# Two fused convolution layers on one core: x1's and x3's stores while layer 0 runs alone, and an image's first value rows

## The chip, the cores and the metric

The kernel runs on one core of a Trainium2 chip. The metric is the device time of one execution in microseconds (us). A profiled execution of the kernel gives the trace that the views below are read from. The engines are named PE (TensorE, matmuls; PEld its weight loads), DVE (VectorE), ACT (ScalarE), POOL (GpSimd) and SP (SyncE, which here only issues DMAs). SPq and ACTq in a view are the queues of instructions of these engines.

## The reference, cut to what matters

Layer 0 normalises each image by groups, makes three 1x1 convolutions of it, computes nine weights per position from two of them, and sums nine shifted copies of the third (x3) with these weights. Layer 1 is local attention over 7x7 windows of keys and values with reflected borders, beside a dynamic 3x3 convolution. Both are added to their input.

```python
# layer 0: x is (8, 256, 64, 64)
x1 = _conv1x1(x, w1, b1); x2 = _conv1x1(x, w2, b2); x3 = _conv1x1(x, w3, b3)
...
w = _conv1x1(h, cw2, cb2).reshape(B, G, K * K, H, W)
x3p = jnp.pad(x3, ((0, 0), (0, 0), (1, 1), (1, 1)))
x3u = _unfold3(x3p).reshape(B, G, SHARE, K * K, H, W)
out = jnp.einsum('bgskhw,bgkhw->bgshw', x3u, w).reshape(B, OUT, H, W)
...
# layer 1, attention part
v = _c1x1(x, Wv, bv).reshape(b * HEAD, HD, h, w)
uv = _unfold(jnp.pad(v, rpad, mode='reflect'), KA).reshape(b * HEAD, HD, kk, n)
...
out_att = jnp.einsum('bnk,bdkn->bdn', att, uv).reshape(b, c, h, w)
...
x = x + _L0_conv_ref(_gn(x), ...)
x = x + _L1_conv_ref(_gn(x), ...)
```

The result of layer 0 with its residual, before layer 1, is called x1 in the kernel (another x1 than in the reference).

## The kernel before, in words

An image has 8 bands of 8 rows; 8 images make 64 bands. The main loop runs over `g` from -12 to 63 and in each over eight steps `s`. In stage `g`, layer 1 works on band `g`, and layer 0 on bands ahead: its 1x1 convolutions on band `g + 12`, its hidden maps on `g + 11`, its products on `g + 10`. For `g < 0` there is no layer 1 work, and layer 0 runs alone: twelve such stages come first (products are in their alone form up to `g = -2`). Image `b + 1` follows image `b` without a break: its first value rows are made in the last stage (`i == NB - 1`) of image `b`, or in stage -1 for the first image.

The order of the instructions is written out by hand. `beside` (L914) puts functions on two lists of a step, `mid` and `end`, which the loop calls at the middle and at the end of it. `steer` (L984) issues most loads at the step's start. `after(n, f)` calls `f` when `n` places have passed; a step has six places. Each engine takes its instructions in the order in which they were written, and an instruction that waits holds all that stand behind it on its engine. SP issues all DMAs of the main loop.

The layer 0 part of a stage, by names and lines:

- `value_maps` (L362) makes x3: PE's matmuls into `p3`, ACT's copy with bias into `x3n` (one buffer for each half of the channels), and a store to DRAM (L375). While alone it is called at s = 2 and s = 3.
- `values_by_group` (L381) loads x3 back by groups into `x3q` (two buffers), five or six DMAs at s = 5, one of which (L397) needs the next band's x3. `x_by_group` (L399) loads the band's x into `xg` by four DMAs at s = 4. `load_x` (L99) fetches x for the convolutions (`xc`, s = 0) and for the statistics of a later image (`xs`, s = 3).
- `tap_weights` (L459) makes the nine products on DVE (L479, tile `prod`, two buffers). While alone, six of them are added into `xg` by POOL (L487) and three are summed by PE (`gather`, L500), and `combine` (L507) on DVE adds PE's sum. `take` (L509) then takes the statistics of the result and stores x1 to DRAM by four DMAs (L519). In the order of the program, `combine` of a band stands on DVE directly behind the first product of the next band, and `take` runs about s = 2 of the next stage.

The layer 1 part that is touched: `load_rows` (L547) loads a band's rows of x1 with three rows above and below, `yp`, and `normalise` scales them on ACT. `values` (L575) makes a tile row of values on PE from them, in two halves, copied by ACT into `vc` (one buffer, L600). `store_values` (L607) stores it to the DRAM tile `vd` (lines L616 to L625), 14 DMAs for the first tile row of an image and 8 for most others. `value_tile` (L627) loads one of four column tiles `vt` (11 buffers) of a tile row from there (L642). For tile rows 0 and 8 the reflected rows have no row of their own in `vd`: each is loaded from the row that it mirrors, so a tile takes 4 x 2 DMAs where others take 2. `weighted_values` (L786) multiplies probabilities by the value tiles on PE, one to two steps after the scores; band `i` needs tile rows `i` and `i + 1`. At an image's boundary, tile row 0 is made at s = 4 and 5 of the last stage and loaded at the end of s = 7; tile row 1 is made at s = 6 and 7 and loaded at the ends of s = 0, 1 and 2 of the next.

Of the kernel before, what the change touches and what calls it, by code (L numbers as in the profile page):

```python
# [18 lines left out]
P = 128  # L19
# [4 lines left out]
R = 8  # L24
BAND = R * W
NB = H // R
# [21 lines left out]
PAD = KA // 2  # L48
WP = W + 2 * PAD
TQ = 8  # L50
# [3 lines left out]
KW = TQ + 2 * PAD  # L54
# [32 lines left out]
def conv_layers_kernel(ctx: ExitStack, tc: tile.TileContext, ins: dict, out: bass.AP):  # L87
    nc = tc.nc
# [48 lines left out]
    x3n = [const.tile([P, R, HP], F32, name=f"x3n_{ct}") for ct in range(NCT)]  # L137
# [72 lines left out]
    images = [Image() for b in range(B)]  # L210
# [148 lines left out]
        if i == NB - 1:  # L359
            nc.gpsimd.tensor_copy(t[0:96, R + 1, :], t[0:96, R - 1, :])  # L360

    def value_maps(b, i, mt):  # L362

        im = images[b]
        if mt == 0:
            im.x3[i] = dram.tile([C, R, HP], F32, tag="x3", name=f"x3_{b}_{i}")
        p3 = ps.tile([P, BAND], F32, tag="gen", name=f"p3_{b}_{i}_{mt}", bufs=4)
        for kt in range(NCT):
            nc.tensor.matmul(  # L369
                p3, im.w3s[:, kt, mt * P : (mt + 1) * P], im.xc[i][:, kt, :],  # L370
                start=(kt == 0), stop=(kt == NCT - 1),
            )
        p3 = p3.rearrange("p (r c) -> p r c", r=R)
        nc.scalar.activation(x3n[mt][:, :, 1 : 1 + W], p3, AF.Identity, bias=im.bias[:, 1 + mt : 2 + mt])
        nc.sync.dma_start(out=im.x3[i][mt * P : (mt + 1) * P], in_=x3n[mt])  # L375

    def pieces(v, q):

# [80 lines left out]
    def tap_weights(b, i, u, alone, at):  # L459


        im = images[b]
        first, n = TG[alone] * u, min(TG[alone], KK - TG[alone] * u)
        pw = ps.tile([P, n, SR * HP], F32, tag="gen", name=f"pw_{b}_{i}_{u}", bufs=4)
        for j in range(n):
            nc.tensor.matmul(  # L466
                pw[:, j], c2[:, first + j], h2n[i % 2].rearrange("p r c -> p (r c)"), start=True, stop=True
            )

        def product(j):  # L470
            k = first + j
            if alone and j == n - 1:
                prod = w1.tile([P, NCT, RP, W], F32, tag="yp", name=f"prod_{b}_{i}_{k}", bufs=3)
                prod = prod.rearrange("p t r c -> p (t r c)")[:, : SHARE * SR * HP]
                prod = prod.rearrange("p (s n) -> p s n", s=SHARE)
            else:
                prod = w0.tile([P, SHARE, SR * HP], F32, tag="prod", name=f"prod_{b}_{i}_{k}", bufs=2)
            at = k // 3 * HP + k % 3
            nc.vector.scalar_tensor_tensor(  # L479
                prod[:, :, :RUN], pw[:, j, :RUN].unsqueeze(1).to_broadcast([P, SHARE, RUN]),  # L480
                par[:, PCB2 + k : PCB2 + k + 1],
                im.x3q[i].rearrange("p s r c -> p s (r c)")[:, :, at : at + RUN], ALU.add, ALU.mult,
            )
            if alone and j == n - 1:
                after(9, lambda: gather(prod))
            else:
                nc.gpsimd.tensor_add(im.xg[i], im.xg[i], rows(prod))  # L487
            if k == KK - 2 + (not alone):
                if alone:
                    after(13, combine)  # L490
                after(14 if alone else 7, take)

        def rows(v):
            return v.rearrange("p s (r c) -> p s r c", c=HP)[..., :W]

        def gather(prod):
            if u == 0:
                im.part = score_tile(f"sum_{b}_{i}").rearrange("p t (s r c) -> p t s r c", r=SR, c=W)
            for t in range(2):
                nc.tensor.matmul(  # L500
                    im.part[:, t], ident, rows(prod)[:, t * SHARE // 2 : (t + 1) * SHARE // 2],
                    start=(u == 0), stop=(u == KK // n - 1),
                )

        def combine():
            x = im.xg[i].rearrange("p s r c -> p (s r c)")
            nc.vector.tensor_add(x, im.part.rearrange("p t s r c -> p (t s r c)"), x)  # L507

        def take():  # L509
            x = im.xg[i]  # L510
            if i == 0:
                im.st1 = stat.tile([P, 2 * NB, 6], F32, tag="st1", name=f"st1_{b}")
            for t in range(2):
                v = x[:, t * SHARE // 2 : (t + 1) * SHARE // 2].rearrange("p s r c -> p (s r c)")
                nc.vector.bn_stats(im.st1[:, 2 * i + t, :], v)
            t = im.x1[i] = dram.tile([C, BAND], F32, tag="x1", name=f"x1_{b}_{i}")
            for q in range(NQR):
                v = x[q * REL : (q + 1) * REL].rearrange("p s r c -> p s (r c)")
                nc.sync.dma_start(out=pieces(t, q), in_=v)  # L519

        for j in range(n):
            after(at[j], lambda j=j: product(j))


    def norm_rows(b):
        im = images[b]
# [80 lines left out]
    def store_values(b, j):  # L607
# [9 lines left out]
        for d in range(1, PAD + 1):  # L617
            for to, c in ((PAD - d, d), (PAD + W - 1 + d, W - 1 - d)):
# [3 lines left out]
                else:  # L622
                    for p in range(2):
                        o = vd[at + p : at + p + 2 * count[p] - 1 : 2, to : to + 1].rearrange("u c n -> c u n")
                        nc.sync.dma_start(out=o, in_=vc[p * W + c : p * W + c + 1, : count[p]])  # L625

    def value_tile(b, j, u):  # L627


        im = images[b]  # L630
        vd = im.vd[j]
        vt = im.vt[j, u] = w1.tile([CHUNK, 2, C], F32, tag="vt", name=f"vt_{b}_{j}_{u}", bufs=11)
        if j == 0:
            runs = [(PAD, PAD, R - PAD)] + [(PAD - d, PAD + d, 1) for d in range(1, PAD + 1)]
        elif j < NB:
            runs = [(0, 0, R)]
        else:
            runs = [(0, 1, PAD)] + [(PAD - 1 + d, PAD - d, 1) for d in range(1, PAD + 1)]
        for to, at, n in runs:
            for g in range(2):  # L640
                c0 = (2 * u + g) * TQ
                nc.sync.dma_start(  # L642
                    out=vt[to * KW : (to + n) * KW, g], in_=vd[at : at + n, c0 : c0 + KW]
                )

    def new_keys(i):

# [266 lines left out]
    def beside(g, s):  # L914

        b, i = divmod(g, NB)
        bn, inx = divmod(g + 1, NB)
        mid, end = [], []
# [15 lines left out]

        made = [(b, i + 2, 4)] if g >= 0 and i < NB - 1 else []
        if i == NB - 1 and 0 <= b + 1 < B:
            made = [(b + 1, 0, 4), (b + 1, 1, 6)]
        for bb, j, d in made:
            if s in (d, d + 1) and (j < NB or s == d):
                mid.append(lambda bb=bb, j=j, d=d: values(bb, j, s - d))  # L940
            if s == d + 1:
                end.append(lambda bb=bb, j=j: store_values(bb, j))
            if s == 7 and d == 4:
                for u in range(NT // 2):
                    end.append(lambda bb=bb, j=j, u=u: value_tile(bb, j, u))
        if g >= 0 and i == 0 and s in (0, 1, 2):
            for u in {0: (0,), 1: (1,), 2: (2, 3)}[s]:
                end.append(lambda u=u: value_tile(b, 1, u))

        nxt = [(b, i + 2, 0)] if g >= 0 and i + 2 < NB else []  # L950
        if i == NB - 1 and 0 <= b + 1 < B:
# [7 lines left out]
        alone = g < 0  # L959
        if 0 <= g + AHEAD < B * NB:  # L960
            bq_, iq = divmod(g + AHEAD, NB)
            if alone and s == 0:
                mid.append(lambda: small_maps(bq_, iq, small_tile(f"{bq_}_{iq}"))())
            if s == (2 if alone else 0):
                (mid if alone else end).append(lambda: value_maps(bq_, iq, 0))
            if s == (3 if alone else 1):
                mid.append(lambda: value_maps(bq_, iq, 1))
        if 0 <= g + AHEAD - 1 < B * NB and s == (2 if alone else 1):
            bh, ih = divmod(g + AHEAD - 1, NB)

# [6 lines left out]
        if 0 <= g + AHEAD - 2 < B * NB and s in TAPS_AT[g < -1]:  # L977
            u = TAPS_AT[g < -1].index(s)
# [5 lines left out]
    def steer(g, s):  # L984

        b, i = divmod(g, NB)
        if s == (2 if g >= 0 else 3) and i == NB - 2 and 0 <= b + 1 < B:
            norm_rows(b + 1)
        n = g + AHEAD + 1
        if s == 2 and n % NB == 0 and 0 < n < B * NB:  # L990
            scaled_weights(n // NB)
        if s == (3 if g < -1 else 7) and g + AHEAD0 < B * NB:
            first_stats(*divmod(g + AHEAD0, NB), n=40 if g < -1 else 9)
        if s == 5 and 0 <= g + 1 < B * NB:
            bn, inx = divmod(g + 1, NB)
            xr = images[bn].xr[inx] = x_tile("xr", bn, inx)
            nc.sync.dma_start(out=xr, in_=images[bn].x1[inx].rearrange("(t p) n -> p t n", p=P))
        if s == (0 if g < 0 else 4) and 0 <= g + 1 + AHEAD < B * NB:
            bn, inx = divmod(g + 1 + AHEAD, NB)
            if inx not in images[bn].xc:  # L1000
                images[bn].xc[inx] = load_x(bn, inx, "xc")
        if s == 5 and 0 <= g - 1 + AHEAD < B * NB:
            values_by_group(*divmod(g - 1 + AHEAD, NB))
        if s == 4 and 0 <= g - 1 + AHEAD < B * NB:
            x_by_group(*divmod(g - 1 + AHEAD, NB), g < -2)

    with tc.manual_schedule():

        for i, use in enumerate(("xc", "xc", "xr", "xr", "xs", None, None, None)):
# [4 lines left out]
            x = first_stats(0, i, use, t)  # L1014
# [167 lines left out]
```

## Time and profile before

| | |
|---|---|
| median of 3 runs | 4012.74 us (4012.72 to 4017.47) |
| the profiled execution | 4010.67 us |
| its span, first to last instruction | 4008.9 us |
| busy: PE, DVE, POOL, ACT | 95%, 85%, 79%, 71% of the span |
| first scores of layer 1 (PE, L737) | at 246.34 us |
| layer 0 alone, 27.0 to 247.7 us: PE, DVE, POOL, ACT busy | 172.4, 158.9, 150.7, 98.4 of 220.7 us |
| layer 0 alone: mean DMA share, traffic | 0.85, 213 GB/s |
| 300 to 700 us: PE busy, DMA share | 391.1 of 400 us, 0.44 |

How to read it: a view gives an instruction by its line in the kernel, engine, operation and tiles, with numbers left out of the tiles' names, so that `x3` and `x1` in DRAM both appear as `x`, and `p3` as `p`; the line tells them apart. In a timeline a row has start, duration, engine, line, operation, `out<-in`, and how many of them were merged (`x4`); square brackets hold the engine's idle time before it and what ended that. In the page's groups the number ahead of the last bar is the busy time, and behind it stands the idle time of the engine before these instructions with its main cause. A DMA row on SPq is the issue; the data land later.

### The profile page before, as it was taken

Reading aid. Unit: us, or ns where it says so; the run is one execution under the profiler, and the core shown is the slowest. Engines: PE = TensorE matmul, PEld = TensorE weight load, DVE = VectorE, ACT = ScalarE, POOL = GpSimd, SP = SyncE. Lnnn points to the kernel's source line nnn. Section 1 sums busy time; section 2 is a strip of 40 time slices with the busy share of each in tenths; the row PEclk is TensorE's granted clock in tenths of the full one; section 3 lists DMA queues with packets and bytes.
Section 4 is the critical chain, followed back from the end, with each engine's and each line's share of the span. In section 5 each row is a group of like instructions: output and inputs, shape, how many; then the busy total and the mean of one; then the engine's idle time right before and its main releaser. Section 6 shows DMA issues by size and latency. Waiting matters only on the chain.

```text
span 4008.9 us, 72420 instructions
## 1 busy us (share of the span) xinstructions
PE 3807.0 (95%) x24620; PEld 2116.9 (53%) x24620; DVE 3419.8 (85%) x7143; ACT 2839.5 (71%) x6779; POOL 3174.8 (79%) x2156
## 2 busy tenths in 40 slices
PE   6879999999999999999999999999999999999998
PEld 3445555555555555555555555555555555555554
DVE  5868988888888988888988888978988889977888
ACT  3457777677676777777777677777777677676776
POOL 4758988788987988878887888978888888965665
PEclk9989999999999999999999999999999999999999
DMA  8864543544444443444443544444443544322220
GB/s 230 201 165 113 134 114 104 136 125 113 127 115 122 124 124 101 125 132 120 124 115 104 138 125 118 110 130 124 118 115 90 129 116 104 85 61 88 71 65 32
DMA packets 493171, 469.42 MB, mean 117 GB/s; under 512 B 68432, under 2 KB 394624, under 8 KB 492544
## 3 DMA queue, kind: packets, MB, share of 16 engines
q1 hardware_dynamic: 489472, 460.23, 43.4%
q10 hardware_dynamic: 3328, 4.55, 0.3%
q8 instruction: 195, 3.19, 0.3%
q14 instruction: 176, 1.44, 0.1%
HBM read 325.64 MB, written 138.99 MB: 116 GB/s over the span
## 4 chain that ended last, share of the span: by engine, by line
PE 27%; POOL 26%; DVE 22%; ACT 10%; issue 7%; DMA 5%; SPq 3%; POOLq 0%; DVEq 0%; ACTq 0%
PE pf L873 13%; POOL xg L487 13%; POOL ex L1080 6%; DVE prod L479 5%; DVE acc L856 5%; DVE rec L894 4%; PE small L786 3%; ACT x L343 3%; PE sco L737 2%; PE ptp L774 2%; ACT ex L878 2%; DVE prob L751 2%; DMA x3q<-x 2%; PE pq L672 2%; DVE acc L830 2%
## 5 line engine op out<-in xcount | busy, mean ns | idle before, releaser
L873 PE MATMUL pf<-yp,c_wfc 128*128 128x512 f32 x4096 | 1917.1, 597 | 6.2 <-ACT ex L878 5.1
L487 POOL TENSOR_TENSOR xg<-xg,prod 128x1024 f32<-128x1024 f32 x549 | 1200.7, 2187 | 177.2 <-DVE prod L479 148.3
L873 PEld LDWEIGHTS pf<-yp,c_wfc 128*128 128x128 f32 x4096 | 744.0, 191 | 730.3 <-issue 647.1
L1080 POOL TENSOR_TENSOR ex<-ex,ex 128x1024 f32<-128x1024 f32 x384 | 907.9, 2364 | 55.9 <-ACT ex L878 51.8
L479 DVE SCALAR_TENSOR_TENSOR prod<-pw,c_par,x3q 128x1040 f32<-128x1040 f32 x576 | 737.9, 1288 | 124.8 <-PE pw L466 56.1
L830 DVE SCALAR_TENSOR_TENSOR acc<-yp,c_chan,acc 128x504 f32<-128x504 f32 (+3 forms) x1104 | 775.0, 702 | 50.7 <-ACT acc L821 30.3
L856 DVE SCALAR_TENSOR_TENSOR acc<-hid,c_chan,acc 128x504 f32<-128x504 f32 (+3 forms) x1024 | 749.8, 732 | 18.1
L878 ACT ACTIVATE ex<-pf 128x512 f32<-128x512 f32 x1024 | 602.1, 588 | 204.2 <-PE pf L873 184.3
L759 ACT ACTIVATE prob<-prob,nmax 128x196 f32<-128x196 f32 x1024 | 459.2, 451 | 217.1 <-DVE nmax L751 216.9
L768 ACT ACTIVATE prob<-prob,tot 128x196 f32<-128x196 f32 x1024 | 413.0, 452 | 235.3 <-DVE tot L766 235.1
L895 POOL TENSOR_TENSOR tot<-tot,rec 128x256 f32<-128x256 f32 x254 | 185.4, 730 | 412.9 <-DVE rec L894 387.9
L894 DVE RECIPROCAL rec<-tot 128x256 f32<-128x256 f32 x256 | 445.9, 1742 | 17.2 <-POOL tot L889 12.3
L776 ACT COPY pt<-ptp 112x512 f32<-112x512 f32 x511 | 294.8, 577 | 123.4 <-PE ptp L774 122.3
L751 DVE CUSTOM_DVE_ANT_0 prob<-sco,c_mask 128x196 f32<-128x196 f32 x1024 | 324.5, 354 | 20.4 <-PE sco L737 20.2
L786 PE MATMUL small<-pt,vt 112*64 112x64 f32 x8144 | 300.3, 226 | 37.5 <-DMA vt<-vd 37.1
L774 PEld LDWEIGHTS ptp<-ident,prob 128*112 128x112 f32 x2044 | 228.1, 134 | 188.9 <-issue 135.2
L774 PE MATMUL ptp<-ident,prob 128*112 128x128 f32 x2044 | 322.9, 281 | 1.3 <-ACT vc L600 1.3
L786 PEld LDWEIGHTS small<-pt,vt 112*64 112x64 f32 x8144 | 261.5, 138 | 116.7 <-issue 75.4
L737 PE MATMUL sco<-kb,qb 64*64 64x196 f32 x4096 | 236.1, 343 | 39.6 <-DVE kb L708 32.9
L592 PE MATMUL pv<-c_wv,yp 128*128 128x256 f32 (+1 forms) x1056 | 252.8, 382 | 2.6 <-ACT ex L878 2.1
L369 PE MATMUL p<-xc,w3s 128*128 128x512 f32 x512 | 248.4, 609 | 7.0 <-ACT ex L878 7.0
L466 PEld LDWEIGHTS pw<-h2n,c_c 128*128 128x128 f32 x1152 | 173.3, 191 | 153.5 <-issue 113.1
(139 smaller groups left out, 4756.9 us busy)
## 6 DMA issues: line engine op xcount, KB each, us to landing
vt<-vd SPq DMA_DIRECT2D x448, 112.0 KB
x<-x3n SPq DMA_DIRECT2D x128, 264.0 KB
x3q<-x SPq DMA_DIRECT2D x128, 264.0 KB
xc<-in_x SPq DMA_DIRECT2D x64, 512.0 KB
xg<-in_x SPq DMA_DIRECT2D x256, 128.0 KB
x<-xg SPq DMA_DIRECT2D x256, 128.0 KB
yp<-x SPq DMA_DIRECT2D x128, 256.0 KB
xr<-x SPq DMA_DIRECT2D x64, 512.0 KB
```

Source lines behind the costliest of these rows:

```text
L479: nc.vector.scalar_tensor_tensor(prod[:, :, :RUN], pw[:, j, :RUN].unsqueeze(1).to_broadcast([P, SHARE, RUN]), par[:, PCB2 + k : PCB2 + k + 1],
L487: nc.gpsimd.tensor_add(im.xg[i], im.xg[i], rows(prod))
L759: nc.scalar.activation(prob[:, h, :NKEY], prob[:, h, :NKEY], AF.Exp, bias=nmax[:, h : h + 1], scale=-1.0, accum_out=tot[:, h : h + 1],)
L768: nc.scalar.activation(prob[:, h, :NKEY], prob[:, h, :NKEY], AF.Copy, scale=tot[:, h : h + 1])
L774: nc.tensor.transpose(ptp[:, h, ch], prob[:, h, ch * CHUNK : (ch + 1) * CHUNK], ident)
L786: nc.tensor.matmul(po[half[h], :, t * TQ : (t + 1) * TQ], im.vt[i + ch, m][:n, t, (2 * ct + h) * HD : (2 * ct + h + 1) * HD], pt[:n, h, ch ...
L830: nc.vector.scalar_tensor_tensor(o, yp[:, ct, ra + dr : rb + dr, ca + dc : cb + dc], chan[:, ct, CW1 + k : CW1 + k + 1], o, ALU.mult, ALU.add,
L856: nc.vector.scalar_tensor_tensor(o, hid[:, ra + dr : rb + dr, ca + dc : cb + dc], chan[:, ct, CW2 + k : CW2 + k + 1], o, ALU.mult, ALU.add,)
L873: nc.tensor.matmul(pf, wfc[:, kt, 2 * m + j, ct * P : (ct + 1) * P], images[b].yp[i][:, kt, PAD : PAD + R], start=(kt == 0), stop=(kt == N ...
L878: nc.scalar.activation(ex[:, j].rearrange("p (r c) -> p r c", r=R), pf, AF.Exp)
L894: nc.vector.reciprocal(rec, v)
L1080: after(4, lambda ex=ex, exb=exb: nc.gpsimd.tensor_add(ex, ex, exb))
```

## The change

- `take` no longer stores x1 itself. The new function `keep` does; while alone it is put on a list `held`, which `steer` empties at s = 6, behind the loads of s = 3, 4 and 5. Otherwise it is called at once, as before.
- For `g < 0`, x3's stores are issued by ACT instead of SP.
- An image's tile rows 0 and 1 of values are made one step sooner (s = 3 and 4, 5 and 6).
- The new function `mirror_rows` copies three rows within the DRAM tile `vd` for tile rows 0 and 8, one step after `store_values`; `value_tile` then loads every tile by two DMAs.
- The tiles of tile row 1 are loaded in the middle of s = 0 and of s = 2, two at a time.

```diff
-    def value_maps(b, i, mt):
+    def value_maps(b, i, mt, alone):
...
-        nc.sync.dma_start(out=im.x3[i][mt * P : (mt + 1) * P], in_=x3n[mt])
+        queue = nc.scalar if alone else nc.sync
+        queue.dma_start(out=im.x3[i][mt * P : (mt + 1) * P], in_=x3n[mt])
...
                 nc.vector.bn_stats(im.st1[:, 2 * i + t, :], v)
+            if alone:
+                held.append(keep)
+            else:
+                keep()
+
+        def keep():
+            x = im.xg[i]
             t = im.x1[i] = dram.tile([C, BAND], F32, tag="x1", name=f"x1_{b}_{i}")
...
+    def mirror_rows(b, j):
+
+        vd = images[b].vd[j]
+        for d in range(1, PAD + 1):
+            to, at = (PAD - d, PAD + d) if j == 0 else (PAD + d, PAD - d)
+            nc.sync.dma_start(out=vd[to], in_=vd[at])
+
     def value_tile(b, j, u):
...
-        if j == 0:
-            runs = [(PAD, PAD, R - PAD)] + [(PAD - d, PAD + d, 1) for d in range(1, PAD + 1)]
-        elif j < NB:
-            runs = [(0, 0, R)]
-        else:
-            runs = [(0, 1, PAD)] + [(PAD - 1 + d, PAD - d, 1) for d in range(1, PAD + 1)]
-        for to, at, n in runs:
-            for g in range(2):
-                c0 = (2 * u + g) * TQ
-                nc.sync.dma_start(
-                    out=vt[to * KW : (to + n) * KW, g], in_=vd[at : at + n, c0 : c0 + KW]
-                )
+        at, n = (0, R) if j < NB else (1, 2 * PAD)
+        for g in range(2):
+            c0 = (2 * u + g) * TQ
+            nc.sync.dma_start(out=vt[: n * KW, g], in_=vd[at : at + n, c0 : c0 + KW])
...
-            made = [(b + 1, 0, 4), (b + 1, 1, 6)]
+            made = [(b + 1, 0, 3), (b + 1, 1, 5)]
...
-            if s == 7 and d == 4:
+            if s == d + 2 and j in (0, NB):
+                end.append(lambda bb=bb, j=j: mirror_rows(bb, j))
+            if s == 7 and j != 1:
...
-        if g >= 0 and i == 0 and s in (0, 1, 2):
-            for u in {0: (0,), 1: (1,), 2: (2, 3)}[s]:
-                end.append(lambda u=u: value_tile(b, 1, u))
+        if g >= 0 and i == 0 and s in (0, 2):
+            for u in (s, s + 1):
+                mid.append(lambda u=u: value_tile(b, 1, u))
...
+        if s == 6:
+            while held:
+                held.pop(0)()
```

## The prediction

> **What bounds the kernel now.** I read the page first, for where TensorE (PE) is not full.
>
> ```profile
> span 4008.9 us, 72420 instructions
> ...
> PE   6879999999999999999999999999999999999998
> ...
> L786 PE MATMUL small<-pt,vt 112*64 112x64 f32 x8144 | 300.3, 226 | 37.5 <-DMA vt<-vd 37.1
> ```
>
> A slice is 100 us. PE is full from the fourth on, so there only PE's idle time can be won; the largest wait is for value tiles, 37.1 us. The first two and a half slices, layer 0 alone, are not full. Next the windows view, cut at the starts of the DVE `combine` (L507), one per alone stage (columns: stretch, length, busy us and instructions of PE, PEld, DVE, ACT, POOL, clock, DMA share, GB/s):
>
> ```profile
> 71.33:90.24 18.91, 14.99 (x71) 6.91 (x70) 16.91 (x15) 7.57 (x15) 14.03 (x12) 0.91 0.87 198
> ...
> 108.81:126.95 18.14, 13.46 (x68) 6.88 (x69) 14.70 (x16) 6.44 (x13) 13.78 (x10) 0.91 0.86 191
> ...
> 182.23:199.93 17.70, 13.23 (x63) 6.36 (x64) 14.69 (x15) 5.21 (x12) 14.23 (x11) 0.81 0.84 192
> 199.93:220.22 20.29, 17.24 (x83) 8.82 (x82) 17.54 (x27) 7.82 (x16) 14.86 (x11) 0.92 0.96 239
> ```
>
> Six stages from 90.24 to 199.93 take 109.69 us, 18.28 each, and no engine is busy over about 15. The timelines of SP's queue and of DVE in one of them say why:
>
> ```profile
> 110.05 2.56 SPq L519 DMA_DIRECT2D x<-xg  x4
> 112.65 0.61 SPq L99 DMA_DIRECT2D xs<-in_x  x1
> 113.36 0.43 SPq L375 DMA_DIRECT2D x<-x3n  x1
> 113.83 2.69 SPq L405 DMA_DIRECT2D xg<-in_x  x4
> ...
> 120.46 0.61 SPq L397 DMA_DIRECT2D x3q<-x  x1
> ...
> 125.73 1.30 DVE L479 SCALAR_TENSOR_TENSOR prod<-pw,c_par,x3q 128x1040 f32<-128x1040 f32 x1 [1.93 <-DMA x3q<-x]
> 126.95 1.21 DVE L507 TENSOR_TENSOR xg<-sco_sum,xg 128x1024 f32<-128x1024 f32 x1
> ```
>
> It is a ring: x1's stores wait for the combine (ended 110.03); xs, x3's store, xg and x3q queue behind them on SP; the first product waits for x3q; the next combine stands behind that product on DVE. Last, the image boundary, SP's timeline and PE's:
>
> ```profile
> 729.30 17.12 SPq L642 DMA_DIRECT2D vt<-vd  x32
> 746.53 1.33 SPq L616 DMA_DIRECT2D vd<-vc  x2
> 747.90 3.83 SPq L621 DMA_DIRECT2D vd<-vc  x6
> 752.41 1.44 SPq L642 DMA_DIRECT2D vt<-vd  x2
> ```
> ```profile
> 755.32 0.55 PE L786 MATMUL small<-pt,vt 112*64 112x64 f32 x8 [2.61 <-DMA vt<-vd]
> ```
>
> The 32 small loads of tile row 0 hold SP for 17 us, so row 1's tiles come too late. The PE waits view, image by image, gives 8.9 us in the first image and 2.9, 4.1, 4.1, 5.1, 3.5, 2.6, 5.8 in the other seven, 28.1 together.
>
> [...] an x3 store costs SP 0.34 us, and the DMA row is full for about 15 of these 18 us. [...] So each row copy holds SP until its source row has landed; before shows the like once, ScalarE's copy waiting 11.87 us for `vd<-vc` at 245.25. [...] No copy within DRAM is in this trace.
>
> **Part 1, x1's stores and x3's stores while layer 0 is alone.** SP's order per stage becomes xc, xs, xg x4, x3q, then x1 x4; ScalarE issues x3's. Removed ahead of x3q: 2.56 + 0.43 us of issue and, more, the wait for the combine. xs then waits only for its statistics (DVE at 122.52), three places before the combine. What is late next? Three candidates.
> - POOL with DVE. From a combine's start: combine, two statistics, two products, then POOL's five adds; at 108.81 the adds began 5.09 us later and took 11.19, so 16.3 and a handover. The stage at 71.33 checks it: 18.91, with one 2.28 us DVE preparation of `c_wfc` in this chain, gives 16.63. I take 16.6.
> - DMA. In the half-microsecond DMA row of 108 to 128 the engines stand at 8 to 9 tenths from about 111.2 to 126: 14.8 us of work per stage. A floor just below, so x3q lands with little to spare: xs, xg, x3q and x3's stores are some 2.4 MB, 10 us at 240 GB/s, with 13 between the statistics and the product after next.
> - PE, 14.4 us dense from its gather at 94.13 to 108.5.
>
> ScalarE gains two issues of 0.34 us and the wait for the end of its own 0.69 us activation: some 2 us on 6 to 10 of 18; the hidden maps queued behind it reach PE's convolution 8 us before PE takes them (108.2 against 116.05). Free.
> Sum: six stages at 16.6, plus 1.5 us for the statistics of the next image inside the one at 145.30 (DVE 16.24 against 14.7), 101.1: **8.6 us off**. Bounds: 0 if DMA, fuller, is late all the same; 14 if POOL's gap closes too. The stage at 199.93 follows the normalisation chain, and stages before 71 wait for weights and the first x3q: nothing.
>
> **Part 2, values one step sooner, first image.** Today the 14 stores of tile row 0 are issued from 233.41 to 244.03, behind x3q; ScalarE's next values copy waits 11.87 us for them, the reflected keys stand behind it, and PE idles 6.45 us at 246.3. A step sooner, the first values matmul waits for the normalised rows (ScalarE, 222.8); the second half follows near 228, the stores run 230 to 240, landing 1.6 (the measured `vd<-vc`), scores at 242.7: **3.6 off** (0 to 6). x3q, now behind the stores, is needed only inside the next stage.
>
> **Part 3, whole-tile loads and copies of reflected rows.** Per image two tile rows go from 32 loads to 8: SP sheds 2 x 24 x 0.54 = 26 us, and gets 2 x 3 copies of 72 KB. A copy's cost has no row: below, 1.6 us to landing; above, on one engine (240/16 = 15 GB/s) 4.9 us each and in series with landings about 23 us for three. [...]
> SP from the end of step 4 at the boundary (708.5 in the trace above: a step before 716.57): stores 9.2, xr and x3q 4.5, copies 5, second stores 5.2, xs and x1 3.3, eight tile loads 5.2, the first four of row 1 2.6, landing 2: all in by about 37 us, near 745. PE wants them at 751.9. The wait goes, with 6 us to spare. What is late next: the values matmul, a step sooner, meets the normalised rows with 1.8 us of slack (ScalarE done at 697.97, PE there at about 699.8), 0 in the last image; I allow 0.5 us per boundary. PE holds the same work otherwise, so idle removed is time removed: 28.1 - 3.5 = **24.6 off**. In the first image the row-1 tiles come some 20.6 us after the first scores against 19.3 wanted: **7.6** of 8.9 off. Bounds for this part: 15 to 37. The earlier place for row 1's loads costs SP at most a wait for the weighing before it, under 1 us in the waits view.
>
> **Sum.** 8.6 + 3.6 + 7.6 + 24.6 = 44.4. Profiled execution: 4010.67 us (span 4008.9 and 1.8 around it), so 3966.3. The median is 2.1 above that execution, so 3968 for a median; I say 3967.
>
> **Rivals.**
> - A, as above: 3967, own range 3952 to 3982. Chance 0.50.
> - B, alone stages unmoved: DMA is the bound (share 0.86), x3q only trades queueing behind x1 for queueing in the DMA engines. For it, the DMA row; against, 2 us of idle rings each stage and 16.6 measured. Only 32 us go: 3980. Chance 0.22.
> - C, more than that: earlier tiles and rows also let ScalarE off its waits for `yp` (63.7 us in all, up to 10.5, behind the same SP bursts), and the alone stages run at 15.5. Another 8 + 10: 3949. Against it, PE shows no wait of that kind. Chance 0.15.
> - D, slower: the row copies hold SP. Three in series on one engine are 23 us, 18 over what I took and 12 beyond the 6 to spare: PE waits 12 us at eight boundaries, 96, against 49 that were to go or came from elsewhere (37.1 + 3.6 + 8.6): +47, 4059. It turns slower when SP is held about 17 us in all (8 x 6.2 against 49). [...] Chance 0.06.
> - E, no change: the boundary wait goes over to another engine and the stages stay: about 4010. Chance 0.07. That the change does not do what it says I see nowhere: the stores are moved only for stages below zero, but tiles and copies work in every image.
>
> A measurement of this kernel tells about 0.2% (8 us) from no change. Faster: A, B, C, 0.87. Same 0.06, slower 0.07. Range 3940 to 3994: A, B, C and what lies between; D and E are left out.
>
> **What would show it.** Right: combines 16.3 to 17 us apart; x1 x4 after x3q on SP; no row L786 waiting for `vt<-vd` over 2 us in all but the first image; vt bursts of 8 in some 5 us; scores of the first band about 12 us sooner. Wrong: products still waiting for x3q (B); a copy taking over 5 us, SP standing before tile loads (D); PE waiting at `pv` for `yp`.

## The result, and the profile after

The changed kernel takes 3972.22 us (median of 4 runs, 3969.72 to 3973.63) against 4012.73 (4 runs of the kernel before beside it, 4010.49 to 4017.47): a ratio of 0.9896, with a 95% interval of 0.988 to 0.9911. The prediction said 3967 with a range of 3940 to 3994. The time came out as predicted; its parts did not. They missed in opposite directions, so that the agreement of the sum is luck. That is what the experiments are about.

The profiled execution took 3969.72 us. The page, in the parts shown of before:

```profile
span 3967.9 us, 71908 instructions
...
PE   5879999999999999999999999999999999999998
...
L795 PE MATMUL small<-pt,vt 112*64 112x64 f32 x8144 | 294.9, 225 | 1.3 <-DMA vt<-vd 0.9
```

The wait for value tiles is gone (37.1 us before, 0.9 now), and the span is 41 us shorter. But in the first of the forty slices PE has fallen from 6 tenths to 5: layer 0's alone part has become slower. To split the two I use PE's first scores of layer 1 (`sco<-kb,qb`), which begin at 246.34 us before and at 254.20 after. Up to there the changed kernel **loses 7.9 us** (predicted: 12.2 won, parts 1 and 2 together). From there to the end of the span it takes 3713.7 us against 3762.6: it **wins 48.9** (predicted: 32.2, part 3). The sum, 41.0, is close to the 44.4 predicted because the two misses, 20.1 and 16.7, nearly cancel.

The stages of the alone part, in the windows view cut at the starts of the DVE `combine` (L508 now; columns as in the prediction):

```profile
93.93:113.24 19.31, 16.50 (x76) 7.52 (x74) 14.71 (x14) 8.96 (x17) 14.47 (x14) 0.91 0.70 190
...
132.57:150.68 18.11, 13.67 (x58) 6.76 (x59) 15.10 (x17) 4.02 (x8) 13.23 (x7) 0.72 0.86 198
150.68:171.57 20.89, 19.07 (x104) 10.14 (x102) 16.23 (x27) 12.37 (x26) 14.37 (x13) 1.00 0.72 186
```

The six stages that took 109.69 us take 115.43, from 93.93 to 209.36. DVE and POOL are busy for the same 13 to 16 us in each, and the DMA share (the last but one column) is lower than before, 0.70 to 0.86 where it was 0.76 to 0.91. So rival B, to which the DMA engines were the bound, does not explain it: something is waiting to issue. The timeline of SP's queue shows where:

```profile
108.23 6.90 SPq L527 DMA_DIRECT2D x<-xg  x4
117.49 0.37 SPq L99 DMA_DIRECT2D xc<-in_x  x1
117.96 0.41 SPq L99 DMA_DIRECT2D xs<-in_x  x1
118.56 2.56 SPq L406 DMA_DIRECT2D xg<-in_x  x4
...
124.43 2.40 SPq L390 DMA_DIRECT2D x3q<-x  x3
```

x1's four stores do stand behind the loads, as intended. But they take 6.90 us where four issues had taken 2.56, and then xc waits until 117.49. What SP waits for is in the waits view of its queue, from 60 to 225 us (columns: us in all, times, longest):

```profile
SPq L527 <- DMA x<-x3n: 30.8, 6, 9.4
SPq L406 <- DMA x<-x3n: 16.4, 4, 5.5
SPq L99 <- DMA x<-x3n: 12.8, 5, 5.0
```

Together 60.0 us, and none of it in the same view of the kernel before. `x<-x3n` is x3's store, which ScalarE now issues. Yet x1's store (L527) reads only xg, and the xg and xs loads (L406, L99) only the input: they have no data in common with x3. In that stage ScalarE's own timeline has:

```profile
111.87 0.33 ACTq L376 DMA_DIRECT2D x<-x3n  x1
...
114.37 0.33 ACTq L376 DMA_DIRECT2D x<-x3n  x1
```

SP goes on two to three microseconds after each of them, at 113.93 and 117.49. The trace shows what joins them: it has the semaphores that are waited for ahead of each DMA, and the one to which the DMA reports its landing. The 2878 DMAs of the changed kernel report to eight semaphores, 100 to 107, and both SP's and ScalarE's are found on all eight. In all 2870 cases in which an earlier DMA had the same semaphore, it had landed before the next was issued. SP takes the eight in turn: 2808 of 2837 steps from one of its DMAs to its next go to the next number. From 60 to 225 us 16 steps leave one out, and these are the 16 numbers that ScalarE's stores of x3 from 77.02 to 208.65 have. An excerpt for the stage above, ScalarE's queue first, then SP's, with the time of issue:

```
L376 x3's store, first half    waits 103, 109 (ScalarE)   reports to 103   111.87
L376 x3's store, second half   waits 105, 109 (ScalarE)   reports to 105   114.37

L527 x1's store, third         waits 103                  reports to 103   113.93
L99  xc                        waits 105, 110 (PE)        reports to 105   117.49
```

In all 15 of the waits summed above, the DMA before which SP stands reports to a semaphore that one of ScalarE's stores of x3 took last, and SP goes on 0.01 to 0.15 us after that store has landed.

My reading: when all of these were on SP, the DMA that had the semaphore last had always been issued, and in most cases had landed: before, 153 of SP's 159 DMAs from 60 to 225 us found it landed, and the other six stood 0.87 us at most for it. Now it may be one that ScalarE has yet to issue, after PE's `p` and its own activation. This is the theory the runs below test: **a ring from SP through the shared semaphores to ScalarE and back**; the way back is through data, from SP's late loads to the products, PE and ScalarE's next store. Its rival: the loss sits at the start, where ScalarE's own loads and first stores are late (`c_mask` is issued at 31.62 us instead of 27.16).

### The profile page after: what moved, and what is told of

The parts are those of the page before. It is cut to its first block, busy times and chain, and to the rows that moved or that the text cites. A ratio compares the mean times of both kernels' runs of the same rounds, so it can differ in the third digit from the quotient of the medians.

```text
span 3967.9 us, 71908 instructions
## 1 busy us (share of the span) xinstructions
PE 3794.4 (96%) x24620; PEld 2111.5 (53%) x24620; DVE 3420.3 (86%) x7143; ACT 2840.7 (72%) x6779; POOL 3172.3 (80%) x2156
## 4 chain that ended last, share of the span: by engine, by line
PE 31%; POOL 28%; DVE 19%; ACT 9%; issue 6%; DMA 4%; SPq 2%; ACTq 0%; POOLq 0%; DVEq 0%
PE pf L882 14%; POOL xg L488 14%; POOL ex L1094 7%; DVE prod L480 5%; DVE rec L903 4%; DVE acc L865 4%; PE small L795 3%; ACT x L343 3%; PE sco L746 2%; PE ptp L783 2%; PE pk L702 2%; PE pq L681 2%; ACT ex L887 2%; POOL tot L898 2%; DMA x<-x3n 2%
## 5 line engine op out<-in xcount | busy, mean ns | idle before, releaser
L746 PE MATMUL sco<-kb,qb 64*64 64x196 f32 x4096 | 235.6, 343 | 35.6 <-DVE kb L717 32.7
```

## The experiments

All twelve were compared with the kernel before on the same chip; differences between kernels of different chips, taken from the medians, agree with those from the ratios within 2 us. The table has what they share: where x3's stores are issued, whether x1's are held, and which of the three edits of the boundary are in (copies with whole-tile loads; values a step sooner; row 1's loads in the middle of the step). Then the median in us with the ratio and its interval, and from each one's profile the six stages of the alone part, the start of the first scores, and the time from there to the end of the span.

| kernel | x3 on | held | copies, sooner, row 1 | median | ratio | six stages | first scores | rest |
|---|---|---|---|---|---|---|---|---|
| before | SP | no | no, no, no | 4012.73 | | 109.7 | 246.3 | 3762.6 |
| after | ScalarE | yes | yes, yes, yes | 3972.22 | 0.9896 (0.988 to 0.9911) | 115.4 | 254.2 | 3713.7 |
| e1_x3_on_sp | SP | yes | yes, yes, yes | 3950.4 | 0.9842 (0.9826 to 0.9859) | 101.5 | 236.9 | 3712.9 |
| e2_x1_not_held | ScalarE | no | yes, yes, yes | 3968.0 | 0.9885 (0.987 to 0.99) | 113.8 | 257.3 | 3709.9 |
| e3_neither | SP | no | yes, yes, yes | 3961.53 | 0.9865 (0.985 to 0.988) | 115.4 | 251.1 | 3710.4 |
| e4_alone_only | ScalarE | yes | no, no, no | 4029.26 | 1.0038 (1.0023 to 1.0053) | 116.6 | 259.6 | 3766.5 |
| f1_no_copies | SP | yes | no, yes, yes | 4030.79 | 1.0042 (1.0028 to 1.0056) | 102.8 | 237.1 | 3791.3 |
| f2_not_sooner | SP | yes | yes, no, yes | 3951.95 | 0.9847 (0.9834 to 0.9861) | 101.3 | 235.8 | 3714.9 |
| f3_vt_late | SP | yes | yes, yes, no | 3949.46 | 0.9841 (0.9827 to 0.9854) | 102.8 | 236.7 | 3711.5 |
| f4_act_later | SP, then ScalarE | yes | yes, yes, yes | 3964.76 | 0.9878 (0.9865 to 0.9892) | 110.2 | 248.3 | 3713.3 |
| g1_copies_alone | SP | no | yes, no, no | 3959.89 | 0.9862 (0.9849 to 0.9876) | 112.2 | 248.1 | 3709.2 |
| g2_held_copies | SP | yes | yes, no, no | 3950.47 | 0.9837 (0.9824 to 0.9851) | 101.4 | 236.5 | 3712.5 |
| g3_held_alone | SP | yes | no, no, no | 4006.59 | 0.9979 (0.997 to 0.9989) | 101.3 | 234.2 | 3769.6 |
| g4_one_on_act | one of each | yes | yes, yes, yes | 3961.84 | 0.9869 (0.9853 to 0.9884) | 109.2 | 241.8 | 3714.2 |

Two things are seen at once. The rest is 3709 to 3715 us wherever the copies are in and 3763 to 3791 where they are not. And the six stages take 101.3 to 102.8 us in exactly the kernels that hold x1's stores and leave x3's on SP. With x1's stores where they were and x3's on SP, the same instructions in the same order gave 109.7, 112.2 and 115.4, so a single profile of that order is good to some 6 us.

### x3's stores back on SP (e1)

```diff
-        queue = nc.scalar if alone else nc.sync
+        queue = nc.sync
```

> The changed kernel with x3's stores back on SP; x1's stores stay held behind the loads. In the changed kernel the first scores of layer 1 begin at 254.2 us, against 246.3 before. Theory 1 (a DMA waits for the completion semaphore of the DMA eight places before it in program order, on whichever queue, so that SP stands until ScalarE has issued x3's store): with all on one queue no such wait is left, combines come 16.5 to 17.5 us apart, first scores at 238 to 243, 3956 to 3962 us. Theory 2 (the DMA engines are full, or holding x1 back is itself harmful): first scores stay at 250 to 256, about 3972.

3950.4 us: 21.8 faster than the change as it was made, and some 6 below the window that theory 1 had set. SP's waits for `x<-x3n` are gone; from 60 to 225 us its view is led by the wait for the data that the store needs:

```profile
SPq L376 <- ACT x3n L374: 60.2, 18, 10.5
```

A wait of 60 us again, but a harmless one: SP stands there with nothing overdue behind it. The stages:

```profile
90.31:106.70 16.39, 13.56 (x65) 6.18 (x64) 14.66 (x14) 6.81 (x13) 13.76 (x11) 0.90 0.83 227
106.70:123.20 16.50, 15.05 (x80) 7.71 (x79) 14.70 (x15) 8.86 (x17) 13.87 (x11) 1.00 0.78 206
```

At 16.4 to 16.9 us they agree with the chain of DVE and POOL that the prediction had worked out (16.6); the one with the next image's statistics takes 18.1, as forecast (16.6 and 1.5). So the forecast of holding x1's stores was right, and moving x3's cost it all and more.

### x1's stores not held, and neither of the two (e2, e3)

```diff
-            if alone:
-                held.append(keep)
-            else:
-                keep()
+            keep()
```

e3 has the edit of e1 as well.

> The changed kernel with x1's stores back in their old place; x3's stores stay on ScalarE. Theory 1 (SP is held through the semaphores of the stores on ScalarE): the stages stay slow, 18.5 to 20 us apart, and the first 65 us stay late too, since ScalarE's stores stand behind the weights there; first scores at 250 to 257, about 3972. Theory 2 (holding x1 back is what harms): first scores at 241 to 246, 3960 to 3964.

> Only the image boundary's part of the change: x1's stores in their old place and x3's on SP. Both theories: stages as before the change (first combine that counts at 90.2 us, six stages in 110), first scores at 242 to 247 by the values made a step sooner, then the main loop 49 us shorter than before the change: 3960 to 3965. If the main loop owed part of its gain to the other two edits it would be above 3972.

3968.0 and 3961.53 us. x3's stores on ScalarE cost 21.8 us where x1's are held, and 6.5 where they are not. Holding x1's wins 11.1 us with x3's on SP (e3 to e1) and loses 4.2 with x3's on ScalarE (e2 to after). The 6.5 and the 4.2 are not shown by themselves, since the intervals of these pairs overlap; but the gain of 11.1 is gone. The two edits, meant to help one another, work against one another; that they lengthen the same ring from two sides is my reading. In e2, too, SP waits for `x<-x3n`, 43.0 us from 60 to 225 (35.6 at x1's stores, 5.1 at xg's loads, 2.3 at L99), though none of these reads x3. e3's first scores come 4.8 us later than before although its stages hold the same instructions up to the last: that is the spread named under the table, and it shows no gain from the step sooner either.

### The alone part only (e4)

The boundary goes back to single-row loads, the old steps for the values and the old places for row 1's loads; what is left is x1's stores held and x3's on ScalarE.

> Only the edits to layer 0 alone: x1's stores held and x3's on ScalarE, with the image boundary as it was before the change. If the parts add: first scores at 252 to 256, value tiles late by 37 us in all again, 4016 to 4022, slower than before by 0.1 to 0.25 per cent. If the time in which layer 0 is alone is made up for in the main loop: 4012.

4029.26 us, slower than before by 0.23 to 0.53%, and 7 us beyond the expected window: the first scores come at 259.6 us, and the rest is not shorter. This half of the change, as it was made, is a loss, and the boundary's gain covers it.

### ScalarE's stores only after the start, and half of them (f4, g4)

```diff
-        queue = nc.scalar if alone else nc.sync
+        queue = nc.scalar if alone and i > 1 else nc.sync
```
```diff
-        queue = nc.scalar if alone else nc.sync
+        queue = nc.scalar if alone and mt == 0 else nc.sync
```

> The changed kernel, but x3's stores of the first image's bands 0 and 1 issue on SP and only those of the later bands on ScalarE. If the loss of x3 on ScalarE is mostly the start (weight loads and c_mask queued behind the first stores, 3.7 us at the first counted combine), it is 3951 to 3957 us. If it is the ring through the shared completion semaphores in every stage, the stages stay at about 19.2 us, the first combine comes back to 90 to 91 us, SP still waits over 25 us for x<-x3n and the time is 3966 to 3971 us.

> The changed kernel with only the first half of x3's stores on ScalarE, the second on SP: half the dose. If SP is held through the completion semaphores that ScalarE's stores share with its own, SP still waits at x<-x3n, about half as long as in the changed kernel (15 to 45 us over the stages against 69), and the time lies between 3950.4 and 3972.2 us, 3955 to 3965. If the loss comes from the second store's lateness in ScalarE's own order alone, the waits at x<-x3n are gone and the time is 3949 to 3953 us; if one store on ScalarE costs as much as two, 3968 to 3973 us.

f4: 3964.76 us, a little under the expected window. The first counted combine comes back to 88.67 us (93.93 after), so the start is a real part of the loss: 7.5 us of the 21.8, more than the 3.7 I had given it. The other 14.4 remain with the ring: SP still waits for `x<-x3n`, 53.1 us from 60 to 240. Nor is the start a cause of another kind. In the changed kernel ScalarE itself stands there for the DMA ahead on the same semaphore: 4.32 us before `c_mask`, until `c_wk` has landed, and 3.79 before x3's second store, until SP's `xs` has.

g4: 3961.84 us, between the two as expected. Its view, 60 to 225 us:

```profile
SPq L527 <- DMA x<-x3n: 25.1, 4, 9.0
SPq L99 <- DMA x<-x3n: 18.6, 3, 7.7
```

That makes 43.7 us, all of them behind the one store that ScalarE issues, against 60.0 with both on ScalarE (the 69 in my expectation was too high). The 4.2 us for `x<-x3n` at L390 are behind the store that SP issues itself. Half the dose gives about half the loss, 11.4 of 21.8 us, but nearly three quarters of the waiting: one store on another engine is enough to break SP's stride.

### The parts of the boundary (f1, f2, f3, g1)

Three kernels with x3's stores on SP and x1's held, each with one edit of the boundary undone. f1 has the single-row loads back and no copies:

```diff
-        at, n = (0, R) if j < NB else (1, 2 * PAD)
-        for g in range(2):
...
+        if j == 0:
+            runs = [(PAD, PAD, R - PAD)] + [(PAD - d, PAD + d, 1) for d in range(1, PAD + 1)]
...
+        for to, at, n in runs:
+            for g in range(2):
...
-            if s == d + 2 and j in (0, NB):
-                end.append(lambda bb=bb, j=j: mirror_rows(bb, j))
```
f2 and f3:
```diff
-            made = [(b + 1, 0, 3), (b + 1, 1, 5)]
+            made = [(b + 1, 0, 4), (b + 1, 1, 6)]
```
```diff
-        if g >= 0 and i == 0 and s in (0, 2):
-            for u in (s, s + 1):
-                mid.append(lambda u=u: value_tile(b, 1, u))
+        if g >= 0 and i == 0 and s in (0, 1, 2):
+            for u in {0: (0,), 1: (1,), 2: (2, 3)}[s]:
+                end.append(lambda u=u: value_tile(b, 1, u))
```

> Built on the kernel with x3's stores on SP and x1's stores held (3950.4 us); only the reflected rows go back to single-row loads from vd, 32 loads at an image's boundary, and the copies are gone. If the single-row loads are what kept vt late (SP's burst of 17 to 18 us before the change), PE's waits for vt come back at the second to eighth image in most part, 20 to 28 us in all, and PE's clock in 730:790 falls below 0.99 again: 3970 to 3980 us. If it is the step sooner that brought the gain, under 8 us are lost and PE waits for vt at most 5 us: 3950 to 3958 us.

> Built on the same kernel; only the first values of the next image go back to steps 4 and 6 (from 3 and 5). If the step sooner carries the gain, 10 to 25 us are lost, PE waits for vt again and ACT for yp less: 3960 to 3975 us. If the row copies alone carry it, the loss is under 5 us: 3950 to 3955 us. For the last stage before the first scores: if the step sooner made it wait for yp there, the first scores come 1 to 3 us earlier than 236.9 us with this edit; if the step was worth the 3.6 us that the prediction gave it, 3 to 4 us later.

> Built on the same kernel; only the loads of tile row 1's vt go back to the ends of steps 0, 1 and 2 (from the middles of 0 and 2). Every theory holds this for the smallest part, since tile row 1 is read only a stage later: 0 to 4 us lost, 3950 to 3955 us. Over 5 us would say that the place of these loads on SP, ahead of the next x1 loads, was a part of the boundary's gain that the prediction did not price.

f2 (3951.95 us) and f3 (3949.46) cannot be told from e1: with the copies in, the step sooner and the place of row 1's loads are worth nothing. f1 lost 80 us, far beyond either expectation, and came out slower than the kernel before. Its timelines of SP's queue and of ScalarE at the second boundary:

```profile
735.43 19.88 SPq L659 DMA_DIRECT2D vt<-vd  x36
755.40 0.41 SPq L563 DMA_DIRECT2D yp<-x  x1
```
```profile
760.21 1.13 ACT L572 ACTIVATE yp<-yp,aff 128x896 f32<-128x896 f32 x1 [10.91 <-DMA yp<-x]
```

What I had missed: the burst does not only make its own tiles late. The next rows of x1 (`yp`) stand behind it on SP, and in f1 row 1's first four loads have moved ahead of them too, 36 in one go. ScalarE waits 10.9 us for `yp` there and 94.2 in all (63.7 before, 6.5 after), PE 51.2 for `vt`. The change, at the same boundary:

```profile
730.20 1.89 SPq L642 DMA_DIRECT2D vd<-vd  x3
...
743.84 9.07 SPq L653 DMA_DIRECT2D vt<-vd  x12
753.01 0.40 SPq L563 DMA_DIRECT2D yp<-x  x1
```

g1 puts it to the proof from the other side: the kernel before, with the copies and whole-tile loads alone.

> The kernel before with the row copies and whole-tile loads and nothing else of the change. If the copies carry the whole gain of the main loop, the time from the first scores to the end is about 3713 us and, with first scores at 246 to 251 us as in the kernel before and in the one with the boundary part alone, it is 3959 to 3966 us. If the step sooner and the place of tile row 1's loads had a share of it, 3970 us or more.

3959.89 us, and the shortest rest of all, 3709.2. The copies alone beat the whole change by 12 us and carry all of the main loop's gain.

### Held alone, and held with copies (g3, g2)

> The kernel before with x1's stores held and nothing else, x3's stores on SP. If the alone stages run as in the kernel with x3 on SP (16.9 us each, first scores near 237 us) and the boundary stays as before (3762.6 us from the first scores), it is 3998 to 4003 us, about 11 us off. If holding x1's stores needs the other edits, 4008 to 4016 us.

> The row copies with whole-tile loads, and x1's stores held, all stores on SP; values and row 1's loads at their old places. If those two edits are worth nothing and nothing of theirs depends on the other, 3946 to 3953 us, as with all of the change but x3's stores (3950.4 us); with both undone there may be a loss of the two together, 3955 to 3965 us, if each was covering for the other.

g3: 4006.59 us, 7.7 off instead of the expected 11. The first scores come at 234.2 us, 12 sooner than before, but 7 us of it are given back in the rest, 3769.6, where PE stands 42.1 us for value tiles. g2: 3950.47. It is the change reduced to two parts, and beats both kernels: by 1.5 to 1.8% the kernel before, by 21.8 us the change.

## Why the prediction came out, point by point

- **Part 1, holding x1's stores: right.** Six stages were to take 101.1 us; with x3's stores on SP they take 101.3 to 102.8. In e1 the stage behind them shortens as well, 18.0 us against 20.3, where I had put nothing. One reading was loose: in the stage at 145.30 PE is busy for 17.18 us, over the "about 15" that I gave for every engine.
- **Part 1, x3's stores on ScalarE: the step that failed.** "ScalarE gains two issues of 0.34 us and the wait for the end of its own 0.69 us activation [...] Free." I counted what is behind the store on ScalarE and not what is behind it on SP. The moved stores still take their turns among the eight semaphores, and SP inherits ScalarE's lateness, 60 us of waits. Cost: 21.8 us, of which f4 puts 7.5 at the start. That the move would do no more than take 0.43 us of issue off SP ahead of x3q was my estimate; it also cost, on the queue that the stores had left.
- **Part 2: not obtained.** PE's wait for the reflected keys did shrink, 6.45 to 2.76 us, but the stage ahead of the first scores lasts 25.28 us against 26.12; undoing the step (f2) costs nothing. The term that failed is "the second half follows near 228", 8 us into the stage. The first values matmul meets rows that are not yet normalised, ahead of `p` and of the taps' matmuls in PE's order. In the changed kernel, PE's timeline:

```profile
229.70 0.70 PE L602 MATMUL pv<-c_wv,yp 128*128 128x256 f32 x2 [1.13 <-ACT yp L572]
231.85 2.93 PE L602 MATMUL pv<-c_wv,yp 128*128 128x256 f32 x6 [1.45 <-ACT yp L572]
```
and the windows view right behind it:
```profile
233.60:238.20 4.60, 4.60 (x9) 2.27 (x9) 0.44 (x1) 0.63 (x1) 3.54 (x2) 0.52 0.08 22
```
PE is busy throughout, at a granted clock of 0.52. The second half of the values comes at 239.13, ten microseconds into the stage. The 14 stores begin at 241.89, 13.0 us into it where before they began 13.2 us into it, and ScalarE's next copy still waits 7.10 us for them.
- **Part 3: the idle time right, the busy time missed.** From the first scores to the end, the two windows, before and after:

```profile
246.34:4008.90 3762.56, 3632.80 (x23788) 2028.85 (x23788) 3246.50 (x6919) 2738.54 (x6590) 3020.94 (x2029) 0.99 0.42 111
```
```profile
254.20:3967.90 3713.70, 3616.84 (x23788) 2020.53 (x23788) 3245.27 (x6919) 2738.58 (x6589) 3020.58 (x2029) 1.00 0.43 114
```
PE's idle time falls from 129.8 to 96.9 us, by 32.9, and the prediction's 24.6 and 7.6 make 32.2. But the same 23788 matmuls are also 16.0 us shorter. "PE holds the same work otherwise, so idle removed is time removed" is the term that was mis-sized: here a stall also cost PE clock behind it. The windows view of before, behind a stall at the second boundary:

```profile
752.00:756.00 4.00, 1.26 (x28) 0.98 (x28) 1.02 (x5) 0.52 (x1) 2.17 (x1) 1.00 0.34 110
756.00:758.00 2.00, 1.83 (x10) 1.18 (x11) 1.45 (x3) 0.00 (x0) 0.00 (x0) 0.84 0.88 235
758.00:760.00 2.00, 2.00 (x4) 0.80 (x3) 1.65 (x3) 1.69 (x2) 1.49 (x1) 0.50 1.03 363
```
PE is idle for 2.7 of four microseconds, and two later it runs at half the clock: four matmuls in 2.00 us. From the first scores on, PE is busy for 39.2 us at half the clock before and for 6.4 after. The difference, 32.8, would take half as long at the full clock: an estimate of 16.4 us, beside the 16.0 measured. From 300 to 4000 us of the kernel before each stretch at half the clock lasts 3.41 or 6.83 us, and at this boundary it came after pauses of PE of which the longest was 2.61 us; what sets its length and its start the traces do not show. In the kernel after, the clock from 700 to 760 us is 1.00 (0.98 before).
- **The row copies: cheaper than taken.** Three issues take 1.89 us in the timeline above, and SP's waits for their source rows come to 7.7 us at all boundaries together, the longest 1.1. By their semaphores, the three issued from 666.23 on landed 2.2 to 2.4 us after their issue, and the first image's three 5.2 to 6.1 us after. I had taken 5 us of SP for three, an estimate with no copy of before to check it; rival D, which needed 17, is out:

```profile
SPq L642 <- DMA vd<-vc: 7.7, 13, 1.1
```
- **Row 1's loads in the middle of the step** were priced at under 1 us, and f3 agrees. That holds only beside the copies: f1, which has these loads and the values' step but not the copies, takes 24.2 us more than g3, which has neither. f1 does not tell which of the two edits costs it; I did not try them apart.
- **The rivals.** B is out: with x3's stores on SP and x1's held, the six stages fall to 101 us. C was right that ScalarE would come off its waits for `yp` (63.7 to 6.5 us), but the stages did not reach 15.5, and the idle time saved was what A had. That the time fell near A's is no proof of A: A's alone part was wrong by 20.1 us one way, its main loop by 16.7 the other.

What stays open is the ring's price in a clean form. That SP waits for ScalarE's stores through the shared semaphores is in the trace; that this is the whole of the 21.8 us rests on e1 and on the dose (f4, g4), since no run kept x3's stores on ScalarE with semaphores of their own.

## What to carry to other kernels

Before moving a DMA to another engine's queue, look up in the trace on what semaphore the DMAs behind it wait: here the queue that had lost two stores a stage waited 60.0 us for the engine that got them. Many small loads in one burst can cost what stands behind them on the queue more than they cost themselves (in f1 ScalarE waited 94.2 us for `yp`, PE 51.2 for the tiles), and here three copies in DRAM that make the source whole, 1.89 us of SP, replaced them. When a stall of PE is removed, look for a lower clock behind it too (here 16.0 us beside 32.9); and when a sum comes out right, compare it term by term at a cut of the trace before believing its parts.

## What the runs showed of the hardware

- SP and ScalarE are not independent as issuers in these programs: SP waited 60.0 us for DMAs that ScalarE issued and with which it shared no data, 43.7 with half as many of them (g4), and not at all with none (e1). In each of the 15 waits of the changed kernel the DMA that waited reported to the semaphore that ScalarE's had taken last. SP issued nothing else while it stood: from 109.45 to 113.93 us x1's last two stores, xc, xs and the xg loads were all behind the one wait.
- The DVE product that reads x3q is shown waiting for x1's store, which it does not read; in the changed kernel's DVE timeline:

```profile
131.35 1.30 DVE L480 SCALAR_TENSOR_TENSOR prod<-pw,c_par,x3q 128x1040 f32<-128x1040 f32 x1 [3.64 <-DMA x<-xg]
```
A load of x3q that it does wait for landed at 131.07, while x1's stores raised the semaphores of two other such loads again up to the product's start. Here the releaser that the view names is only the one that last raised a count.
- Three copies of 72 KB within DRAM in a row held their queue for 1.89 us (from 730.20); all 48 landed 2.1 to 7.1 us after their issue, and a tile load that reads them waited at most 1.1 us.
- Seven times between 300 and 4000 us in the kernel before, PE ran at half the clock for 3.41 or 6.83 us; in the 3.41 us ahead of each it had been idle for 1.6 to 3.4 us. In this kernel that added about half as much again to what the stalls themselves cost (16.0 us beside 32.9).
